# A decoder layer on one core: sends paced in fours, a quarter of the dense expert moved to the front, and a closing sum made by VectorE alone

## The chip, the core and the metric

The kernel runs on 1 core of a Trainium2 chip. The metric is the device time of one execution in microseconds (us); the time of a kernel is the median of its runs.

A core has five engines with a queue of instructions each: TensorE (PE in the profile, with its weight loads as PEld), VectorE (DVE), ScalarE (ACT), GpSimd (POOL) and SyncE (SP), which here only issues transfers. Matrix products land in PSUM; everything else lies in SBUF or in device memory (DRAM). Each queue is worked off in order, and an instruction whose input is not there holds up all that stand behind it.

## The reference, cut to what matters

One decoder layer over 16 x 64 = 1024 tokens of width 256, in float32: self-attention, cross-attention over a second sequence, and a mixture of experts, each behind a layernorm and added to x. Only the last part is touched:

```
xt = layernorm(x)                              # 1024 tokens x 256
scores = softmax(xt @ Wg.T)                    # 16 experts in 4 groups
best 2 groups by their maximum, in them the best 4 experts: topi, weights
h = silu(xt @ W1[e].T) * (xt @ W3[e].T)        # 176 wide, for each expert e
expert_out[e] = h @ W2[e].T
y = sum over e of expert_out[e] * combine[:, e]    # 0 where e was not chosen
z = (silu(xt @ Ws1.T) * (xt @ Ws3.T)) @ Ws2.T      # the shared expert, 352 wide
x = x + y + z
```

## The kernel before

**Tokens and tiles.** x stays in SBUF as eight tiles of 128 tokens (`x[0]` to `x[7]`, pairs in one buffer), or two halves of 512 tokens. A float32 product is made of three: each operand is split in a high part (a cast, by ScalarE) and a low part (the difference, by VectorE or GpSimd); `parts_of` makes both, at lines 112 and 113. Every matrix product of this part goes through the helper at line 104.

**Routing through DRAM.** Experts 0 to 14 take only tokens that chose them; 15, the last, is computed densely for all tokens. For each token tile and each of four choices, `send` (line 842) issues one indirect transfer on GpSimd that scatters 128 rows to slots of the DRAM table `xd`, 384 slots for an expert. That is 4 choices x 4 tiles x 2 halves = 32 sends. The framework would order writes to one table one behind the other; `side_by_side` declares each send independent of the ones before it. Expert e's load of its rows waits only for the sends of choices 0 to e (of all four from e = 3 on), since `expert_inputs` asks for `sent_for[k]` of those choices.

**One expert** (loop over e at the end of `decoder_layer`):
- `expert_weights`: SyncE loads 640 KB; ScalarE casts the high part (line 278), VectorE makes the low part (line 283), helped by GpSimd from e = 3 on. At most two raw weight tiles are alive.
- `expert_inputs`: SyncE loads 384 rows (tile `xr`, line 1255), PE transposes them (1265), `parts_of` makes `xs`.
- `expert_hidden`: 18 products of 384 columns ("up products"), silu (ScalarE, 1283 and 1286), product (VectorE, 1284 and 1287), parts `hp`.
- `send_outputs`: 15 products of 256 columns, copies to `y` (1299), three indirect transfers on GpSimd that scatter rows to the DRAM table `yd` (1304), by token and choice.

For e = 1 and 2 the hidden layer of expert e - 1 is put ahead of the inputs of expert e; later the inputs come first, so that PE always has an expert's rows ready. Weights of expert e are issued behind the last silu issued so far (`tc.issue_after(silus[-1])`); such calls only bind the order in which instructions are placed, and a scheduler with a model of its own places the rest. The order in each queue is then fixed.

**The dense expert.** Its weights are `w_last`. Half 0 is computed with the shared expert before the loop. Half 1 comes in two quarters of 256 tokens: `dense_hidden` (18 products of 256 columns and the steps of a hidden layer) and `dense_output` (10 products and two adds to x at line 952, `add_last`). Both quarters stand at the end: hidden of the first before expert 14's outputs, the rest after them.

**The end.** `load_outputs(k)` loads the rows of choice k from `yd`, four loads of 256 KB on SyncE (line 1320, tile `got`, nine buffers), once the sends that can hold rows of it have landed: choice 0 after expert 11, choice 3 after expert 14. `add_outputs` multiplies each of the eight tiles with its weight and adds it to x: two of three tiles by one VectorE instruction (line 1334), every third by ScalarE (1331, the multiplication) and GpSimd (1332, the addition). Then x goes out, eight stores, in turn from SyncE and ScalarE (1392).

Of the kernel before, what the change touches and what calls it, by code (L numbers as in the profile page):

```python
# [29 lines left out]
AF = mybir.ActivationFunctionType  # L30
ALU = mybir.AluOpType
# [11 lines left out]
E, INTER, NGRP, TOPK, TOPKG = 16, 176, 4, 4, 2  # L43
# [28 lines left out]
def decoder_layer(ctx: ExitStack, tc: tile.TileContext, a: dict, out: bass.AP):  # L72
    nc = tc.nc
# [17 lines left out]
    def av_tile():  # L91
        return ps_av.tile([128, 512], F32, tag="av", name="av")
# [18 lines left out]
    def parts_of(src, hi, lo, eng=None):  # L111
        nc.scalar.copy(hi, src)  # L112
        return (eng or nc.vector).tensor_tensor(lo, src, hi, ALU.subtract).ins
# [3 lines left out]
    x = [t[:, i, :] for t in x_pairs for i in range(2)]  # L117
# [122 lines left out]

    yd = dram.tile([(E - 1) * SLOTS + TOPK * NT, D], F32, tag="yd", name="yd")

    def side_by_side(sent, others):

        for other in others:
            tc.declare_no_dep(sent, other, reason="each writes rows of its own")
        others.append(sent)

    def behind(read, writes):
        for w in writes:  # L250
            tc.add_manual_dep(
                read,
                w.name,
                mybir.DependencyInfo(mybir.DependencyClass.Sync, mybir.DependencyReason.DATA),
                reason="it reads rows of each",
            )
# [29 lines left out]
    def expert_up(w, xs, n):  # L286


        ps = [mm_tile(cols=n) for _ in range(3)]
        return ps, [expert_up_part(k, w, xs, t) for k, t in enumerate(ps)][-1]  # L290
# [24 lines left out]
    with ExitStack() as attn:  # L315
# [410 lines left out]
        rows = [None, None]  # L726
        sent_rows, sent_for = [], [[] for _ in range(TOPK)]
# [108 lines left out]

        def send(half, choices=range(TOPK), waits=()):

            to = targets[half]
            for k in choices:  # L840
                for i in range(4):
                    sent = nc.gpsimd.indirect_dma_start(
                        out=xd[: TOPK * NT + (E - 1 - k) * SLOTS],
                        out_offset=bass.IndirectOffsetOnAxis(ap=to[:, k, i : i + 1], axis=0),
                        in_=rows[half][i // 2][:, i % 2, :],
                        in_offset=None,
                    ).ins
                    side_by_side(sent, sent_rows)
                    sent_for[k].append(sent)
                    behind(sent, waits)  # L850

# [107 lines left out]
        with (  # L959
# [109 lines left out]
            def dense_weights():  # L1069

                parts = [
                    xw.tile([128, 2, 2, 4 * HQ], F32R, tag=f"w_q{n}", name=f"w_last{n}")
                    .rearrange("p a b c -> p (a b c)")[:, :W_COLS]
                    for n in range(2)
                ]
                up = xb.tile([128, 3, 2, 2, DC], F32, tag="w_s", name="w_last_up")
                down = xb.tile([128, 2, D], F32, tag="w_o0", name="w_last_down")
                for t, cols in (
                    (up.rearrange("p a b c d -> p (a b c d)"), slice(0, W_UP)),
                    (down.rearrange("p a b -> p (a b)"), slice(W_UP, W_COLS)),  # L1080
                ):
                    nc.sync.dma_start(out=t, in_=a["W123"][E - 1][:, cols])
                    parts_of(t, parts[0][:, cols], parts[1][:, cols])
                return parts
# [18 lines left out]
            def dense_gated(g, up, g2, up2):  # L1103
                h_p = [
                    xa.tile([128, 512], F32R, tag=f"roped1{n}", name=f"dense1{n}", bufs=1)
                    for n in range(2)
                ]
                h_p.append(xa.tile([128, 512], F32R, tag="q_r", name="dense2"))
                nc.vector.tensor_tensor(g, up, g, ALU.mult)
                parts_of(g, h_p[0], h_p[1])  # L1110
                nc.vector.tensor_tensor(g2[:64], up2[64:], g2[64:], ALU.mult)
                parts_of(g2[:64], h_p[2][:64], h_p[2][64:])
                return h_p
# [15 lines left out]
            for n in range(len(units) + 2):  # L1129
# [5 lines left out]
                qd, half = units[min(n, len(units) - 1)]  # L1135
# [52 lines left out]
                if n == 8:  # L1188
                    w_last = dense_weights()
                    with after(exps[-1]):  # L1190
                        routed.append(weights_of_choices(0))
                if n == 9:
# [30 lines left out]
                    with after(aimed, placed):  # L1223
# [4 lines left out]
                        h_p = dense_gated(*dense_ups)  # L1228
# [9 lines left out]
    gated, up_done = [None], [None]  # L1238
# [34 lines left out]
    def expert_hidden(w, xs, n):  # L1273


        ps, up_done[0] = expert_up(w, xs, n)
        g, h, g2, h2 = (
            fh.tile([128, SLOTS], F32, tag=tag, name=tag)[:, :n] for tag in ("g", "h", "g2", "h2")
        )
        h_p = [  # L1280
            fh.tile([128, SLOTS], F32R, tag=tag, name=tag)[:, :n] for tag in ("hp0", "hp1", "hp2")
        ]
        nc.scalar.activation(g, ps[0], AF.Silu)
        nc.vector.tensor_tensor(h, ps[1], g, ALU.mult)
        parts_of(h, h_p[0], h_p[1])
        silus.append(nc.scalar.activation(g2[64:], ps[2][:64], AF.Silu).ins)
        nc.vector.tensor_tensor(h2[:64], ps[2][64:], g2[64:], ALU.mult)
        gated[0] = parts_of(h2[:64], h_p[2][:64], h_p[2][64:])
        return h_p
# [24 lines left out]
    def load_outputs(k):  # L1314

        tiles = []
        for n in range(NI // 2):
            t = fy.tile([128, 2, D], F32, tag="got", name="got", bufs=9)
            first = (E - 1) * SLOTS + (TOPK - 1 - k) * NT + n * 256
            got = nc.sync.dma_start(  # L1320
                out=t, in_=yd[first : first + 256].rearrange("(i p) d -> p i d", p=128)
            ).ins
            behind(got, returned)
            tiles.append(t)
        return tiles

    def add_outputs(k, got, cw):
        for i in range(NI):
            y, w = got[i // 2][:, i % 2], cw[i // 4][:, k, i % 4 : i % 4 + 1]
            if i % 3 == 2:  # L1330
                nc.scalar.activation(y, y, AF.Copy, scale=w)
                nc.gpsimd.tensor_tensor(x[i], x[i], y, ALU.add)
            else:
                nc.vector.scalar_tensor_tensor(x[i], y, w, x[i], ALU.mult, ALU.add)  # L1334

    def dense_hidden(w, half, n):
        return expert_hidden(w, [p[:, :, n * 256 : n * 256 + 256] for p in normed[half]], 256)

    def dense_output(w, h_p, half, n, add):
        for b in range(2):  # L1340
            ps = av_tile()[:, :D]
            expert_output(ps, w, h_p, slice(b * 128, b * 128 + 128))
            add(half, 2 * n + b, ps)
# [6 lines left out]
    ws, xs, hs, got = {}, {}, {}, {}  # L1350
    with tc.issue_after(lows[-1]), tc.issue_after(silus[-1]):
        ws[0] = expert_weights(a["W123"][0], nc.vector)
    for e in range(E + 1):
        if e in (1, 2):

            low = lows[-1]
            hs[e - 1] = expert_hidden(ws[e - 1], xs[e - 1][0], SLOTS)
        if e < E - 1:
            low = lows[-1]
            with tc.issue_after(up_done[0] if e in (1, 2) else low):  # L1360
                xs[e] = expert_inputs(e)
            if e >= 1:
                with tc.issue_after(low), tc.issue_after(silus[-1]):
                    ws[e] = expert_weights(a["W123"][e], nc.vector if e < 3 else nc.gpsimd)
        if e == 1:
            with tc.issue_after(gated[0]), tc.issue_after(silus[-1]):
                routed.append(weights_of_choices(1))
        if 0 <= e - 1 < E - 1 and e > 2:
            hs[e - 1] = expert_hidden(ws[e - 1], xs[e - 1][0], SLOTS)
        if e - 2 >= 0:  # L1370
            if e == E:

                with tc.issue_after(gated[0]):
                    h_p = dense_hidden(w_last, 1, 0)
            last = send_outputs(e - 2, ws.pop(e - 2), hs.pop(e - 2), xs.pop(e - 2)[1])
            if e - 2 == E - TOPK - 2:
                short = slots_are_short()
            k = e - 2 - (E - 1 - TOPK)
            if k >= 0:
                got[k] = load_outputs(k)  # L1380
    with ExitStack() as behind_last:
        for ins in (*last, gated[0]):
            behind_last.enter_context(tc.issue_after(ins))
        cw = [r[0] for r in routed]
        add_outputs(0, got[0], cw)
        dense_output(w_last, h_p, 1, 0, add_last)
        add_outputs(1, got[1], cw)
        dense_output(w_last, dense_hidden(w_last, 1, 1), 1, 1, add_last)
        for k in range(2, TOPK):
            add_outputs(k, got[k], cw)  # L1390
    for i in range(NI):
        (nc.sync if i % 2 == 0 else nc.scalar).dma_start(
# [10 lines left out]
    with tc.If(short > 0):  # L1403
        w_over = [weights_without_slot(half, routed[half][2]) for half in range(2)]
        with tc.For_i(0, E - 1, 1) as e:
            w = expert_weights(a["W123"][bass.ds(e, 1)].rearrange("o p c -> p (o c)"))
# [109 lines left out]
```

## Time and profile before

| what | us |
|---|---|
| median of 3 runs (572.08 to 573.05) | 572.2 |
| the profiled execution, its own time | 577.4 |
| its span | 575.5 |
| PE busy | 540.3 (94%) |
| DVE busy | 400.2 (70%) |
| ACT busy | 279.3 (49%) |
| POOL busy | 230.6 (40%) |
| mean granted clock of PE | 0.978 of full |

A line of the order of time gives the start, the time, the engine, the line of the kernel, the operation, what is written and read, how many follow each other, and in brackets how long the engine had been idle and what ended that. The durations in the trace come from one execution, which took 5.2 us more than the median. Transfers that an engine only issues don't count as its busy time.

### The profile page before, as it was taken

The page shows a single profiled execution, that of the slowest core. Times are in us where ns is not written, and L with a number is a line of the kernel's source. Part 1 is how long each engine was busy: PE and PEld are TensorE (multiplying, and loading weights), DVE is VectorE, ACT ScalarE, POOL GpSimd, SP SyncE. Part 2 cuts the span into 40 slices and gives each one's busy share as a digit, 9 for nine tenths or more (in the row PEclk, how much of TensorE's full clock was granted, in tenths as well). Part 3 has the DMA queues.
Part 4 walks back from the last instruction along what each step waited for, and adds up shares of the span by engine and source line. Part 5 has one row for each costly group of instructions (what it writes and reads, how often), then busy time and mean ns, then how long its engine had stood idle before and what let it go on. Part 6 is the DMA issues. An engine that isn't in the chain of part 4 may idle for free.

```text
span 575.5 us, 10603 instructions
## 1 busy us (share of the span) xinstructions
PE 540.3 (94%) x4013; PEld 446.7 (78%) x4013; DVE 400.2 (70%) x879; ACT 279.3 (49%) x524; POOL 230.6 (40%) x213
## 2 busy tenths in 40 slices
PE   7999999999999989999999999999999779999962
PEld 5889898888989876757778577685787669999951
DVE  6355566644655788848577586889777479999866
ACT  4677557575574431230432323152525187777551
POOL 4260500101001005426243444632544717888862
PEclk9999999999999999999999999999999789999995
DMA  8564431823200599482020000000511658777384
GB/s 227 145 166 146 111 109 39 227 86 112 75 1 1 167 250 308 111 239 52 2 70 1 8 1 1 0 31 0 188 50 68 202 169 285 240 245 238 122 279 152
DMA packets 56294, 70.83 MB, mean 123 GB/s; under 512 B 13872, under 2 KB 42768, under 8 KB 56240
## 3 DMA queue, kind: packets, MB, share of 16 engines
q1 hardware_dynamic: 51408, 58.71, 34.5%
q0 software_dynamic: 3696, 10.36, 4.7%
q10 hardware_dynamic: 1136, 1.05, 0.6%
q8 instruction: 33, 0.54, 0.4%
q14 instruction: 21, 0.17, 0.1%
HBM read 48.61 MB, written 21.86 MB: 122 GB/s over the span
## 4 chain that ended last, share of the span: by engine, by line
PE 81%; DVE 7%; issue 4%; DMA 3%; ACT 3%; POOL 1%; SPq 1%; DVEq 0%; ACTq 0%; POOLq 0%
PE mm L104 47%; PE mm L1005 7%; PE av L590 5%; PE av L104 5%; PE at L573 4%; PE at L343 3%; PE at L1028 2%; PE av L1041 2%; PE at L1265 2%; PE mm L439 2%; DMA bqkv<-in_bqkv 1%; PE mm L461 1%; DMA got<-yd 1%; DVE x L1334 1%; POOL roped L990 1%
## 5 line engine op out<-in xcount | busy, mean ns | idle before, releaser
L990 POOL TENSOR_TENSOR roped<-rt,rt 128x512 f32<-128x512 f32 x48 | 62.6, 1325 | 83.4 <-DVE rt L984 80.5
L984 DVE TENSOR_TENSOR rt<-mm,rope_q 128x512 f32<-128x512 f32 x96 | 61.4, 685 | 24.3 <-PE mm L104 23.6
L104 PE MATMUL mm<-xn,w_q 128*128 128x512 f32 x288 | 73.9, 403 | 0.5 <-ACT xn L222 0.5
L104 PEld LDWEIGHTS mm<-xn,w_q 128*128 128x128 f32 x288 | 52.2, 188 | 14.0 <-issue 1.8
L104 PE MATMUL mm<-xs,w 128*128 128x384 f32 x270 | 55.3, 354 | 7.0 <-ACT xs L112 5.8
L1304 POOL DMA_INDIRECT yd<-y,to x45 | 47.9, 1064 | 27.6 <-ACT y L1299 13.1
L104 PEld LDWEIGHTS mm<-xs,w 128*128 128x128 f32 x270 | 48.4, 198 | 9.0 <-ACT xs L112 6.6
L327 ACT ACTIVATE p<-p 128x512 f32<-128x512 f32 x32 | 20.1, 629 | 62.3 <-DVE p L326 62.3
L324 DVE TENSOR_REDUCE sm_m<-at 128x8 f32<-128x512 f32 x32 | 21.8, 680 | 37.1 <-PE at L573 36.2
L1005 PE MATMUL mm<-roped,w_s 128*64 128x512 f32 x192 | 46.4, 602 | 0.7 <-POOL roped L990 0.7
L522 POOL TENSOR_TENSOR wv<-code,scale 128x512 fp32r<-128x512 f32 x7 | 9.5, 1360 | 88.2 <-DMA scale<-in_scales 58.7
L613 DVE TENSOR_TENSOR x<-mm,x 128x256 f32<-128x256 f32 x64 | 26.0, 419 | 23.9 <-PE mm L104 21.9
L104 PE MATMUL mm<-wo,o 128*128 128x256 f32 x256 | 39.6, 295 | 0.0
L104 PE MATMUL av<-w,hp 128*128 128x256 f32 x225 | 35.2, 290 | 0.7 <-ACT y L1299 0.7
L104 PE MATMUL mm<-xn,wq 128*128 128x512 f32 x128 | 34.6, 405 | 0.7 <-ACT xn L222 0.5
L104 PE MATMUL mm<-wv,xn 128*128 128x256 f32 x256 | 35.2, 289 | 0.0
L104 PE MATMUL mm<-xn,wk 128*128 128x512 f32 x128 | 34.9, 404 | 0.0
L590 PE MATMUL av<-pt,v 128*128 128x128 f32 x256 | 34.5, 277 | 0.0
L104 PEld LDWEIGHTS mm<-wo,o 128*128 128x128 f32 x256 | 32.9, 190 | 1.5 <-issue 0.4
L590 PEld LDWEIGHTS av<-pt,v 128*128 128x128 f32 x256 | 32.0, 191 | 1.2
L104 PEld LDWEIGHTS mm<-wv,xn 128*128 128x128 f32 x256 | 31.8, 189 | 0.9
L104 PEld LDWEIGHTS av<-w,hp 128*128 128x128 f32 x225 | 30.6, 190 | 1.9 <-ACT y L1299 1.2
(216 smaller groups left out, 1145.8 us busy)
## 6 DMA issues: line engine op xcount, KB each, us to landing
w<-in_W SPq DMA_DIRECT2D x15, 640.0 KB
code<-in_codes SPq DMA_DIRECT2D x32, 256.0 KB
scale<-in_scales SPq DMA_DIRECT2D x32, 256.0 KB
xr<-xd SPq DMA_DIRECT2D x15, 408.0 KB
xd<-zeros SPq DMA_DIRECT2D x8, 720.0 KB
yd<-zeros SPq DMA_DIRECT2D x8, 512.0 KB
got<-yd SPq DMA_DIRECT2D x16, 256.0 KB
wq<-in_Wq SPq DMA_DIRECT2D x4, 512.0 KB
```

The lines of the kernel that those rows point to most:

```text
L104: m = nc.tensor.matmul(ps, lhsT=l, rhs=r, start=(n == 0), stop=(n == len(pairs) - 1))
L324: nc.vector.tensor_reduce(m, sc, AX.X, ALU.max)
L327: exps.append(nc.scalar.activation(p, p, AF.Exp, scale=scale).ins)
L343: last = nc.tensor.transpose(ps[:, 2 * n : 2 * n + 2, :].rearrange("p a q -> p (a q)"), pn[:, 2 * n : 2 * n + 2, :].rearrange("p a k -> p ...
L439: nc.tensor.matmul(ps[:, c * DCQ : (c + 1) * DCQ], lhsT=wq[:, h, c * 128 : (c + 1) * 128], rhs=wkq[:, h, :], start=True, stop=True,)
L573: nc.tensor.matmul(sc[par * 64 : par * 64 + 64, 2 * g + pp, :], lhsT=qk[0][:, b * S : (b + 1) * S], rhs=qk[1][:, b * S : (b + 1) * S], sta ...
L590: nc.tensor.matmul(av[:, k * 128 : (k + 1) * 128], lhsT=v[:, i, k0 : k0 + HD], rhs=pt[:, i].rearrange("p a q -> p (a q)"), start=True, sto ...
L613: nc.vector.tensor_tensor(x[i], ps, x[i], ALU.add)
L984: nc.vector.tensor_tensor(mt, ps3, rope_table(t, 2 * ab + k), ALU.mult)
L990: nc.gpsimd.tensor_tensor(r.rearrange("p (b s) -> p b s", s=S), one, two, op)
L1005: nc.tensor.matmul(ps[h // 2][(h % 2) * 64 : (h % 2) * 64 + 64], lhsT=w_s[:, t, blk, ab, :], rhs=roped[2 * t + ab], start=first[h], stop=l ...
L1304: sent = nc.gpsimd.indirect_dma_start(out=yd[: (E - 1) * SLOTS + min(TOPK, E - 1 - e) * NT], out_offset=bass.IndirectOffsetOnAxis(ap=to[:, ...
```

## The change

- `send`: for half 1 and choices 1 to 3, each of the four sends keeps its dependence on the last send before the four. It waits until that one has landed. (The sends of half 0, and choice 0 of half 1, are as before.)
- The loop: expert 2's hidden layer also comes ahead of expert 3's inputs, so expert 3's rows are used later.
- The first quarter of half 1 of the dense expert: its hidden layer is placed behind expert 0's up products, its output products and adds ahead of expert 0's outputs. Only the second quarter is left at the end, its hidden layer before expert 14's outputs, its output after them.
- `add_outputs`: all eight tiles by VectorE's one instruction; no ScalarE multiplication, no GpSimd addition.
- `load_outputs`: of the last choice, two of the four loads are issued by ScalarE instead of SyncE.

```
-    def side_by_side(sent, others):
+    def side_by_side(sent, others, landed=()):
         for other in others:
-            tc.declare_no_dep(sent, other, reason="each writes rows of its own")
+            if other not in landed:
+                tc.declare_no_dep(sent, other, reason="each writes rows of its own")
         others.append(sent)
...
             for k in choices:
+                landed = sent_rows[-1:] if half and k else ()
                 for i in range(4):
...
-                    side_by_side(sent, sent_rows)
+                    side_by_side(sent, sent_rows, landed)
...
-            got = nc.sync.dma_start(
+            got = (nc.scalar if k == TOPK - 1 and n % 2 else nc.sync).dma_start(
...
     def add_outputs(k, got, cw):
         for i in range(NI):
             y, w = got[i // 2][:, i % 2], cw[i // 4][:, k, i % 4 : i % 4 + 1]
-            if i % 3 == 2:
-                nc.scalar.activation(y, y, AF.Copy, scale=w)
-                nc.gpsimd.tensor_tensor(x[i], x[i], y, ALU.add)
-            else:
-                nc.vector.scalar_tensor_tensor(x[i], y, w, x[i], ALU.mult, ALU.add)
+            nc.vector.scalar_tensor_tensor(x[i], y, w, x[i], ALU.mult, ALU.add)
...
     for e in range(E + 1):
-        if e in (1, 2):
+        if e in (1, 2, 3):
             low = lows[-1]
             hs[e - 1] = expert_hidden(ws[e - 1], xs[e - 1][0], SLOTS)
+            if e == 1:
+                with tc.issue_after(up_done[0]):
+                    h_p = dense_hidden(w_last, 1, 0)
         if e < E - 1:
             low = lows[-1]
-            with tc.issue_after(up_done[0] if e in (1, 2) else low):
+            with tc.issue_after(up_done[0] if e in (1, 2, 3) else low):
                 xs[e] = expert_inputs(e)
...
-        if 0 <= e - 1 < E - 1 and e > 2:
+        if 0 <= e - 1 < E - 1 and e > 3:
             hs[e - 1] = expert_hidden(ws[e - 1], xs[e - 1][0], SLOTS)
         if e - 2 >= 0:
             if e == E:
                 with tc.issue_after(gated[0]):
-                    h_p = dense_hidden(w_last, 1, 0)
+                    h_p = dense_hidden(w_last, 1, 1)
+            if e == 2:
+                dense_output(w_last, h_p, 1, 0, add_last)
             last = send_outputs(e - 2, ws.pop(e - 2), hs.pop(e - 2), xs.pop(e - 2)[1])
...
-        add_outputs(0, got[0], cw)
-        dense_output(w_last, h_p, 1, 0, add_last)
-        add_outputs(1, got[1], cw)
-        dense_output(w_last, dense_hidden(w_last, 1, 1), 1, 1, add_last)
-        for k in range(2, TOPK):
+        dense_output(w_last, h_p, 1, 1, add_last)
+        for k in range(TOPK):
             add_outputs(k, got[k], cw)
```

## The prediction

> **What bounds the kernel now.** I read the page first, for the share of each engine in the chain that ended last; then busy time by stretches of ten microseconds from 430 us on, because every edit lies in the mixture-of-experts part; then the order of time around the start of the experts and around the end; last the two programs' orders of instructions, engine by engine.
>
> ```profile
> span 575.5 us, 10603 instructions
> ...
> PE 540.3 (94%) x4013; PEld 446.7 (78%) x4013; DVE 400.2 (70%) x879; ACT 279.3 (49%) x524; POOL 230.6 (40%) x213
> ...
> PE 81%; DVE 7%; issue 4%; DMA 3%; ACT 3%; POOL 1%; SPq 1%; DVEq 0%; ACTq 0%; POOLq 0%
> ```
>
> TensorE is the bound as a whole. By stretches:
>
> ```profile
> 480.00:490.00 10.00, 10.00 (x74) 10.00 (x73) 9.18 (x17) 8.40 (x18) 6.63 (x7) 1.00 0.83 277
> ...
> 530.00:540.00 10.00, 10.00 (x67) 9.66 (x66) 9.36 (x17) 6.38 (x16) 8.68 (x7) 1.00 0.39 141
> ...
> 560.00:570.00 10.00, 3.21 (x10) 2.36 (x10) 9.84 (x19) 2.59 (x6) 4.05 (x5) 0.50 0.62 195
> ```
>
> The columns are length, then PE, weight loads, DVE, ACT, POOL, the granted clock, DMA share and GB/s. From 475 to 550 PE has no room: whatever makes the experts start later comes through one to one. After 560 DVE is the full engine. So there are two places to cost: the start of the experts, and the end. The start, in order of time:
>
> ```profile
> 454.54 4.82 PE L104 MATMUL mm<-xs,w 128*128 128x384 f32 x18 [1.45 <-ACT xs L112]
> ...
> 459.19 0.82 PE L1265 MATMUL at<-ident,xr 128*128 128x128 f32 x6
> ...
> 460.57 0.48 ACT L1286 ACTIVATE g<-mm 64x384 f32<-64x384 f32 x1 [1.33 <-PE at L1265]
> 461.08 1.26 ACT L278 CAST w<-w 128x1280 fp32r<-128x1280 f32 x1
> ...
> 462.37 1.56 DVE L283 TENSOR_TENSOR w<-w,w 128x768 fp32r<-128x768 f32 x2 [0.72 <-ACT w L278]
> 462.70 0.48 ACT L112 CAST xs<-at 128x384 fp32r<-128x384 f32 x1 [0.37 <-remote]
> ...
> 463.24 0.79 PE L104 MATMUL mm<-xs,w 128*128 128x384 f32 x3 [3.23 <-ACT xs L112]
> ...
> 463.96 0.56 DVE L113 TENSOR_TENSOR xs<-at,xs 128x384 fp32r<-128x384 f32 x1
> ...
> 464.57 3.25 PE L104 MATMUL mm<-xs,w 128*128 128x384 f32 x9
> ...
> 471.41 0.80 PE L104 MATMUL mm<-xs,w 128*128 128x384 f32 x3 [1.10 <-ACT xs L112]
> ...
> 472.70 0.95 POOL L1304 DMA_INDIRECT yd<-y,to  x1 [11.50 <-ACT y L1299]
> ```
>
> Expert 0's 18 up products end at 459.4. Expert 1's begin at 463.2 and in bulk at 464.6: PE stands for 3.23 us while ACT makes g2 of expert 0, casts w1 (1.26 us), then xs, and DVE makes w1's low part (1.56 us), then xs's. Expert 2 has such a hole of 1.10 us. The clock, us by us:
>
> ```profile
> 450.00:451.00 1.00, 0.32 (x2) 0.32 (x3) 1.00 (x3) 0.00 (x0) 0.85 (x1) 0.91 0.41 148
> ...
> 464.00:465.00 1.00, 0.91 (x6) 0.71 (x5) 1.00 (x3) 0.98 (x2) 0.00 (x0) 0.73 0.36 78
> 465.00:466.00 1.00, 1.00 (x4) 1.00 (x4) 0.97 (x3) 0.68 (x1) 0.00 (x0) 0.50 0.93 307
> ```
>
> It halves twice, 450.8 to 457.6 and 464.5 to 467.9, each time after a thin stretch. The end:
>
> ```profile
> 552.59 3.65 DVE L1334 SCALAR_TENSOR_TENSOR x<-got,cw,x 128x256 f32<-128x256 f32 x9
> ...
> 558.62 0.85 DVE L1334 SCALAR_TENSOR_TENSOR x<-got,cw,x 128x256 f32<-128x256 f32 x1 [2.38 <-DMA got<-yd]
> ...
> 561.20 1.42 DVE L1334 SCALAR_TENSOR_TENSOR x<-got,cw,x 128x256 f32<-128x256 f32 x2
> ...
> 563.39 1.83 DVE L1334 SCALAR_TENSOR_TENSOR x<-got,cw,x 128x256 f32<-128x256 f32 x2
> ...
> 566.12 0.51 ACT L1331 ACTIVATE got<-got,cw 128x256 f32<-128x256 f32 x1 [1.00 <-DMA got<-yd]
> ```
>
> Nine adds follow each other in 3.65 us, so one per 0.40. Later the same form takes 0.7 to 1.0 where POOL adds beside it. DVE ends at 571.2; stores and closing take 4.3 more.
>
> **The end, step by step.** DVE's 18.6 us from 552.6 to 571.2 are: 24 choice adds and 4 dense adds at 0.40 (11.2); four steps of the second quarter's hidden layer at 0.42 (1.7); 2.4 waiting for a load; and some 3.2 of instructions stretched beside POOL (0.85 for 0.40; 1.42 and 1.83 for 0.80; a hidden step of 0.97 for 0.42; about 0.5 in the last rows). Sum 18.5. The change adds 8 choice adds, removes 2 dense adds and the four hidden steps, and takes POOL away: 34 at 0.40 is 13.6, so DVE could end at 566.2. It is then not DVE but the last choice's loads that end last. They wait for expert 14's sends (SyncE issues from 561.0 to 562.9); the third has landed at 566.1, the fourth, issued 0.46 later, by about 566.7 (estimate). Two adds more: 567.6 against 571.2, a gain of 3.6. I take 3.5. The range is 2.0 (the loads come 1.5 later) to 5.0 (the sends leave earlier, as 18 products no longer follow expert 14's outputs on PE). The nine load buffers cost nothing: the last load needs the 24th DVE instruction, 552.6 + 9.5 = 562.1, no later than its issue now. ACT's eight multiplies (0.51 each) and POOL's eight adds (0.78) go from engines with room.
>
> [...] The four issues stand 0.46 apart, while the transfers run until 566.7. [...] By the issue rows alone the fourth load could gain 0.9[...]. I take 0.
>
> **The quarter of the dense expert.** Its 18 up products (2.3 us in the trace, before 554.9) now stand between expert 0's and expert 1's transposes. That looks like PE's hole, but on ACT the cast of w1 waits for the last silu issued, which is now the quarter's own g2: ACT's order is g, g2, hp, g (dense), hp, g2 (dense), then the cast, one dense cast (0.41), xs. So the cast follows the 18 products instead of running beside them. The bulk of expert 1's products moves from 464.6 by 2.3 + 0.4 to 467.3: most of the hole moves instead of being filled. What lies behind on DVE is w1's low part and one dense step, and PE waits for both.
>
> How late they end depends on the clock. Before: 9 products at half clock (3.25 us), then 6 in 1.2, end 469.2. After: 15 products from 467.3. [...] 15 at 0.175 is 2.6, end 469.9, or +0.7. The row disagrees: at 450.8 the clock halved after one 1.6 us gap, and it stayed halved past 454 although about 60% of those 3.4 us were busy. The stretch 464.5 to 467.9 will hold some 2.2 busy us of 3.4, so I take half clock for one more stretch, to 471.3: 11 products at 0.36, 4 at 0.18, end 472.1, or +2.9. If the clock returns at 467.9 it is +1.1. Range 0.7 to 2.9; I take the row.
>
> The quarter's ten output products (five took 0.75) run beside the waits for xs. Its two adds (0.48 each) stand on DVE ahead of w2's low parts; PE has 12 output products meanwhile: +0.4 (0 to 1).
>
> **Fourth rows later.** Expert 2's up products now come before expert 3's transposes, so expert 3 gets a hole as experts 1 and 2 have: ACT g, g2, cast of w3, xs in a row. Nothing in the trace shows it at expert 3; nearest are 1.10 at expert 2 and 3.23 at expert 1, with 8 output products to fill. I take 1.5, near the first of the two (0 to 3.2).
>
> **Sends in fours.** Twelve sends of half 1 wait on POOL for the landing of the last send of the choice before. Before, 16 leave 1.27 us apart until 461.2. A landing takes 2.0 us (the first choice: POOL done 444.5, read at 446.5) to 3.7 (the third: 456.1, 459.8), so three waits put the end near 469 to 470. Behind them POOL has nothing until 472.7, idle for 11.5: that cover hides it. On SyncE w2's load moves ahead of expert 1's rows, which leave near 454.7 instead of 452.4 and land before 460, for a use after 461.6. Expert 2's rows leave near 463 (459.8), used at 472. Expert 3's leave near 471 (463.5), used after 478, and behind them w3, at 471.5 (464.4), cast near 479. I cost all at 0 (below nothing by up to 1, if thinner DMA traffic helps; above by up to 3, if w3 or rows come late, each us one to one).
>
> **Sum.** Start +2.9 + 0.4 + 1.5 = +4.8; end -3.5; together +1.3. Against the profiled execution, 575.5 span and 577.4 in all, that is 576.8 and 578.7. The profiled run is 5.2 above the median of 572.2; I carry the difference over: 573.5.
>
> **The rivals.** (1) The clock decides the other way: it returns at 467.9, or never drops. The start costs 1.1 + 0.4 + 1.5 = 3.0 or, with no drop, 2.6; the end gives 3.5 to 5: 0.5 to 2.4 faster, 569.8 to 571.7, middle 570.8. For it: the dense products do thicken the stretch before; against it: the two drops in the rows. It decides if expert 1's products end before about 470.8 (469.2 and the 1.6 that the other terms leave of the 3.5). (2) The last loads bind harder: on the busy DMA (0.9 and more from 553 to 560) DVE waits longer for them and the end gives only 2: +2.8, 575.0. For it: DVE already waits 2.38 there. (3) The fours bring w3 or the rows late: +3 on top, 576.5. Against it: covers of 7 us. (4) The two queues and the fours do nothing that can be seen; this is in the sum already.
>
> **How the numbers follow.** Forecast 0.44, rival 1 0.34, rival 2 0.13, rival 3 0.09. The forecast's own range is 572 to 575; about a third of it and a little of rival 1 lie within 0.2% (1.1 us, about what a measurement of this kernel tells from no change). So faster 0.33, same 0.18, slower 0.49. Cases of both signs are in: 569.5 to 576.8 leaves out the far ends of rivals 1 and 3.
>
> **What would show it.** Right: the cast of w1 stands behind the dense g2 on ACT, PE's hole before expert 1 is still about 3 us in all, the clock is at 0.50 beyond 468, expert 14's sends end 4 to 6 us after 557.1, DVE runs at 0.40 per add with no stretched rows, and its last add comes about 10.5 us after expert 14's last send, not 14. Wrong: expert 14's sends end within 2 us of 557.1 (the start is too dear in my sum), or the last adds wait for loads by more than 3 us (the end is too cheap).

## The result, and the profile after

| what | before | after |
|---|---|---|
| median, us (7 runs each, one chip) | 572.29 | 575.66 |
| ratio, 95% interval | | 1.0056 (1.0037 to 1.0075) |
| the profiled execution, own time, us | 577.4 | 574.3 |
| its span, us | 575.5 | 572.5 |

The change costs 3.2 us (0.0056 of 572.3). The forecast was slower, 573.5 with a range of 569.5 to 576.8, so sign and range hold; the size does not (1.3 us forecast). But the two traces say the opposite of the medians: the one of after is 3.0 us shorter. Before's trace lies 5.1 us above its median, after's 1.3 below. This is the first thing to clear up. From the page of after:

```profile
span 572.5 us, 10584 instructions
...
PE 535.1 (93%) x4013; PEld 441.3 (77%) x4013; DVE 401.6 (70%) x887; ACT 275.7 (48%) x516; POOL 226.2 (40%) x205
...
PE 75%; DMA 7%; POOL 6%; issue 5%; DVE 4%; ACT 2%; SPq 0%; DVEq 0%; POOLq 0%; ACTq 0%
```

DMA and POOL have 13% of the chain that ended last, where before they had 4%: landings of transfers and the sends now stand on the path. By stretches of 10 us, PE is as full as before in the middle. After 560 it does nothing, and DVE is no longer full (6.63 of 10 us, 9.84 before):

```profile
480.00:490.00 10.00, 10.00 (x73) 9.93 (x72) 8.74 (x17) 8.83 (x20) 7.09 (x7) 1.00 0.90 305
530.00:540.00 10.00, 10.00 (x69) 9.97 (x69) 9.75 (x18) 7.05 (x17) 8.74 (x7) 1.00 0.39 136
560.00:570.00 10.00, 0.00 (x0) 0.00 (x0) 6.63 (x17) 0.00 (x0) 0.00 (x0) 0.50 0.75 246
```

The start of the experts after the change, in order of time:

```profile
455.28 2.31 PE L104 MATMUL mm<-xn,w_last 128*128 128x256 f32 x18
...
457.63 0.38 ACT L1290 ACTIVATE g<-mm 64x256 f32<-64x256 f32 x1 [0.44 <-issue]
...
457.91 0.85 PE L1269 MATMUL at<-ident,xr 128*128 128x128 f32 x6 [0.32 <-DMA xr<-xd]
458.03 1.26 ACT L280 CAST w<-w 128x1280 fp32r<-128x1280 f32 x1
...
461.86 2.87 PE L104 MATMUL mm<-xs,w 128*128 128x384 f32 x15
...
466.26 0.84 PE L1269 MATMUL at<-ident,xr 128*128 128x128 f32 x6 [1.53 <-DMA xr<-xd]
...
469.81 1.14 POOL L1308 DMA_INDIRECT yd<-y,to  x1 [2.15 <-ACT y L1303]
```

The quarter's 18 products follow expert 0's at once. The cast of w1 stands on ScalarE behind the quarter's g2 (457.63), as predicted, and the bulk of expert 1's products starts at 461.86. New is the 1.53 us that PE stands for expert 2's rows at 466.26. The clock by the same microseconds that were shown of before:

```profile
450.00:451.00 1.00, 0.83 (x6) 0.64 (x6) 1.00 (x4) 0.25 (x1) 0.70 (x2) 1.00 0.14 48
464.00:465.00 1.00, 0.73 (x5) 0.41 (x3) 0.71 (x4) 0.89 (x1) 0.89 (x1) 1.00 0.88 272
465.00:466.00 1.00, 0.00 (x0) 0.00 (x0) 0.07 (x1) 0.96 (x3) 0.69 (x2) 1.00 0.95 362
```

It is full throughout the start, even in a microsecond in which PE does nothing. The end:

```profile
551.52 2.86 DVE L1334 SCALAR_TENSOR_TENSOR x<-got,cw,x 128x256 f32<-128x256 f32 x7
...
555.13 0.96 POOL L1308 DMA_INDIRECT yd<-y,to  x1 [0.30 <-issue]
...
561.12 0.88 DVE L1334 SCALAR_TENSOR_TENSOR x<-got,cw,x 128x256 f32<-128x256 f32 x2 [1.10 <-DMA got<-yd]
562.20 5.77 DVE L1334 SCALAR_TENSOR_TENSOR x<-got,cw,x 128x256 f32<-128x256 f32 x14 [0.20 <-DMA got<-yd]
```

Seven adds take 2.86 us and fourteen 5.77: 0.41 each, nothing is stretched any more. DVE's last add ends at 567.97, 11.9 us after expert 14's last send (556.09). DVE stands for loads at 561 and still has 14 adds to do from 562.2 on.

### The profile page after: what moved, and what is told of

Read it like the earlier page. It is cut to its first block, busy times and chain, and to the rows that moved or that the text cites. A ratio compares the mean times of both kernels' runs of the same rounds, so it can differ in the third digit from the quotient of the medians.

```text
span 572.5 us, 10584 instructions
## 1 busy us (share of the span) xinstructions
PE 535.1 (93%) x4013; PEld 441.3 (77%) x4013; DVE 401.6 (70%) x887; ACT 275.7 (48%) x516; POOL 226.2 (40%) x205
## 4 chain that ended last, share of the span: by engine, by line
PE 75%; DMA 7%; POOL 6%; issue 5%; DVE 4%; ACT 2%; SPq 0%; DVEq 0%; POOLq 0%; ACTq 0%
PE mm L104 43%; PE mm L1009 7%; PE av L592 5%; POOL xd L846 4%; PE av L104 4%; PE at L575 4%; PE at L345 2%; PE at L1032 2%; PE mm L441 2%; PE av L1045 2%; DMA got<-yd 2%; DMA xd<-rows,to 2%; PE at L1269 1%; DMA x<-in_x 1%; PE mm L463 1%
## 5 line engine op out<-in xcount | busy, mean ns | idle before, releaser
L104 PEld LDWEIGHTS mm<-xn,w_q 128*128 128x128 f32 x288 | 52.2, 188 | 14.1 <-issue 1.8
L104 PE MATMUL mm<-xs,w 128*128 128x384 f32 x270 | 53.1, 341 | 3.7 <-issue 2.2
L104 PEld LDWEIGHTS mm<-xs,w 128*128 128x128 f32 x270 | 45.7, 188 | 5.7 <-issue 3.2
```

The lines of the kernel that those rows point to most:

```text
L104: m = nc.tensor.matmul(ps, lhsT=l, rhs=r, start=(n == 0), stop=(n == len(pairs) - 1))
```

## The experiments

**How the traces are compared.** Everything before the first send of half 1's rows (call it S) is the same in all kernels, but differs between the chips used by some 2 us (S at 436.7 to 439.6). So times are counted from S, in two pieces. The first runs from S to expert 14's first send to `yd`; it is called the start, since the middle runs alike (54.8 to 56.0 us from expert 4's first send to expert 14's in all traces). The second, the end, runs from there to the end of the span. The last column is PE's time at half clock between S and 482. Times are in us.

| kernel | ratio to before | 95% interval | S to expert 14 | end | half clock |
|---|---|---|---|---|---|
| before, first trace | | | 113.18 | 22.97 | 10.2 |
| before again | 0.9997 | 0.9989 to 1.0006 | 108.77 | 22.32 | 0 |
| after, first trace | 1.0056 | 1.0037 to 1.0075 | 112.54 | 20.36 | 0 |
| after again | 1.0054 | 1.0033 to 1.0074 | 113.55 | 21.15 | 3.4 |
| before + VectorE's adds | 1.0009 | 0.9992 to 1.0026 | 111.29 | 22.06 | 6.8 |
| before + later fourth rows | 1.0032 | 1.0019 to 1.0045 | 111.32 | 22.01 | 3.4 |
| before + early quarter | 1.0046 | 1.0029 to 1.0063 | 111.58 | 22.97 | 3.4 |
| before + fours | 1.0107 | 1.0086 to 1.0128 | 115.17 | 22.23 | 10.2 |
| after - fours | 1.0044 | 1.0029 to 1.0060 | 112.05 | 21.23 | 0 |
| after - early quarter | 1.0039 | 1.0027 to 1.0051 | 110.52 | 23.30 | 3.4 |
| after - later rows | 1.0059 | 1.0040 to 1.0079 | 115.81 | 20.82 | 3.4 |
| after - fours - quarter | 1.0051 | 1.0033 to 1.0069 | 109.82 | 23.01 | 0 |
| after - second queue | 1.0058 | 1.0039 to 1.0077 | 113.49 | 19.18 | 3.4 |
| after - fours, cast of w1 first | 1.0047 | 1.0026 to 1.0068 | 112.86 | 21.33 | 3.4 |

A trace is one execution, and most executions of a kernel lie within 1 to 2 us of their median, a few further off. The ratios carry the verdicts; the traces show the places.

**Before again.** No edit.

> The kernel before, unchanged, for a second trace of it. The profiled execution of before (577.4 us) lies 5.1 above its own median, that of after (574.3) 1.4 below its. Theory A: the two half-clock stretches at 450.8-457.6 and 464.5-467.9 belong to that one execution; a new one has full clock until the end, a span near 570 to 571, sends of expert 14 that end near 552 to 553 and a last add near 566. Rival: the stretches are in every execution of before and the new trace repeats them (span 575, sends end at 557). The ratio is 1.000 within 0.2%.

Theory A held, on a chip on which everything lies 2.4 us earlier. The trace of before, a second time, at the start and one of the microseconds shown earlier:

```profile
453.40 1.26 ACT L278 CAST w<-w 128x1280 fp32r<-128x1280 f32 x1
453.87 0.85 PE L1265 MATMUL at<-ident,xr 128*128 128x128 f32 x6 [1.01 <-DMA xr<-xd]
...
456.89 1.84 PE L104 MATMUL mm<-xs,w 128*128 128x384 f32 x9 [0.55 <-DVE xs L113]
...
458.81 1.21 PE L104 MATMUL mm<-xs,w 128*128 128x384 f32 x6
...
464.56 0.96 POOL L1304 DMA_INDIRECT yd<-y,to  x1 [6.20 <-ACT y L1299]
```

```profile
465.00:466.00 1.00, 0.83 (x8) 0.63 (x7) 1.00 (x3) 0.00 (x0) 0.69 (x2) 1.00 0.95 311
```

Nine products of expert 1 take 1.84 us, not 3.25, and expert 14 is reached 108.77 us after S instead of 113.18. The 4.4 us that the first trace lost are not a property of the kernel. The medians of before on the chips used are 569.8 to 572.7. Less 1.8 outside the span, less S and an end of 22.3, the usual execution of before needs 108.7 to 109.4. The mean granted clock says the same: it was 0.978 in the first trace, and of the 92 other executions of before and of before again two have 0.978 or less; their median is 0.984.

Not all of the 4.4 us is the clock's. Before it halved at 450.8, the first trace was already late:

```profile
449.55 0.48 DVE L952 SCALAR_TENSOR_TENSOR x<-av,cl,x 128x256 f32<-128x256 f32 x1 [3.07 <-PE mm L104]
...
450.68 1.13 PE L104 MATMUL mm<-ws,sh 96*128 96x256 f32 x4 [1.65 <-issue]
```

This add of VectorE reads dense products that began at 446.77, 2.78 us before it. In before again the same add comes 0.79 us after their begin (445.20 and 444.41). Behind it VectorE makes the low part of `sh` until 450.63, and PE stands 1.65 us before the products that read it. Expert 0's products begin 15.1 us after S, against 11.7 in before again. How much of the loss is this late add and how much the half clock that followed is not shown.

Against before again the two traces of after lose 3.8 and 4.8 us at the start and gain 2.0 and 1.2 at the end.

**After again.** No edit.

> After, unchanged, for a trace beside the other parts on one chip. From the parts so far (without the fours 1.0044, without the early quarter 1.0039) I expect 1.0056, that is 573.0 where before is 569.8, the first send of expert 0's outputs some 2.6 later after the first send of half 1's rows than in before, and the last add 11.9 after expert 14's last send. Rival: on this chip the change costs nothing at the start and the ratio is 1.000.

1.0054, as expected. The two traces of after differ in two places: this one has a half-clock stretch late in the start, from 477 (the start is 1.0 us longer), and it takes 12.6 us from the last send to the last add, where the first took 11.9.

**The early quarter**, out of after, and alone on before (with the old adds, all in one run at the end):

```
-            if e == 1:
-                with tc.issue_after(up_done[0]):
-                    h_p = dense_hidden(w_last, 1, 0)
...
-            if e == 2:
-                dense_output(w_last, h_p, 1, 0, add_last)
```

> After, with both quarters of the dense expert at the end as before, all adds on VectorE still. Theory A: 18 products at 0.13 and 10 at 0.15 (3.8 us) leave the start, where they run beside waits only in part, and w1's cast no longer stands behind the dense g2: the experts begin 2 to 3 us sooner; VectorE then has 40 steps in the end in place of 34 (+2.4), but the loads of the last choice come sooner too; net 0 to 1 us faster than after, ratio 1.004 to 1.0056. Rival (the quarter is what pays, it fills a hole): 2 us slower than after, ratio 1.009.

> Before, with the early quarter of the dense expert alone (the old adds of three engines, one queue, no fours, rows as before). Theory A (3.7 us of TensorE's work go to where TensorE is the bound and about 1.3 of them fill a stand; the end gives 1.2 to 2 back): expert 4's outputs leave 56.1 us after the first send, no half clock at the start; ratio 1.000 to 1.002. Rival (the quarter is most of the 3.3 us lost): 1.004 to 1.005.

Out of after: 1.0039, about 1 us less than 1.0055 and just under what theory A allowed; the intervals overlap, so this difference is not clear of noise. Alone: 1.0046, 2.6 us slower, and the rival's number, not the one I had put first. At the start PE was at half clock once, from 465, where I had expected none. What I had wrong is the end, which gives nothing at all (22.97) when ScalarE and GpSimd still add. The order of time at the end of before with the early quarter alone:

```profile
562.39 0.51 ACT L1335 ACTIVATE got<-got,cw 128x256 f32<-128x256 f32 x1 [1.17 <-DMA got<-yd]
...
563.03 0.73 POOL L1336 TENSOR_TENSOR x<-x,got 128x256 f32<-128x256 f32 x1 [0.82 <-ACT got L1335]
563.09 1.34 DVE L1338 SCALAR_TENSOR_TENSOR x<-got,cw,x 128x256 f32<-128x256 f32 x2 [0.21 <-DMA got<-yd]
```

All three engines stand for the same loads, GpSimd by way of ScalarE: with DVE lightened, the loads bind the last adds. Yet these end 12.6 us after expert 14's last send, about as in after (11.9 and 12.6) and earlier than in before (14.1 and 13.7). The time is lost behind them. Each engine's queue closes with an instruction that the trace records as DRAIN and that the views leave out. GpSimd's ends 6.4 us or more after its last work in all fourteen traces. Here it runs from 564.12 to 570.48, while SyncE's, behind its waits for the stores, is over at 567.68; the span ends at 571.3. In the two traces of before GpSimd's DRAIN ends 0.5 and 0.9 us ahead of SyncE's, and in after, where GpSimd does not add, 9.3 us ahead. So with GpSimd still adding, the early quarter moves the adds forward but not the end.

**The adds on VectorE alone**, on before:

```
-            if i % 3 == 2:
-                nc.scalar.activation(y, y, AF.Copy, scale=w)
-                nc.gpsimd.tensor_tensor(x[i], x[i], y, ALU.add)
-            else:
-                nc.vector.scalar_tensor_tensor(x[i], y, w, x[i], ALU.mult, ALU.add)
+            nc.vector.scalar_tensor_tensor(x[i], y, w, x[i], ALU.mult, ALU.add)
```

> Before, with all adds on VectorE and nothing else. The prediction put the end at 3.5 less, of which the quarter (six VectorE steps, 2.5 us) leaves only with the early quarter. Theory A (the last choice's loads and VectorE's 40 steps bind equally; POOL's contention gone is worth what eight more adds cost, 3.2): same as before, ratio 0.999 to 1.001. Rival (contention with POOL is dear, as the prediction's sum has it): 1 to 2 us faster, ratio 0.997.

1.0009: nothing that can be told from no change. This fits theory A (eight more adds on DVE, 3.2 us, cost what is gained where DVE's instructions are no longer stretched beside GpSimd's, some 3.2 us in the first trace of before), but it does not separate the two. So each half of the end's change is worth nothing alone. With the adds on VectorE but both quarters at the end, the last add still comes 12.9 to 14.4 us after the last send (three traces); with the quarter early but GpSimd adding, GpSimd's DRAIN holds the end. Only with both does the end become shorter: 19.2 to 21.3 us in six traces, against 22.0 to 23.0 in the four with the end of before, 1.7 us between the means.

**The later fourth rows**, alone on before, and out of after:

```
-        if e in (1, 2):
+        if e in (1, 2, 3):
...
-        if 0 <= e - 1 < E - 1 and e > 2:
+        if 0 <= e - 1 < E - 1 and e > 3:
```

(and the same in the condition for `up_done`).

> Before, with the later place of the fourth rows alone. Theory A (hidden: in the part that has it without fours and quarter, expert 4's outputs leave 53.9 us after the first send of half 1, as in the undisturbed trace of before, 53.75): 1.000. Rival (the prediction's 1.5 us for a hole before expert 3): 1.0026; with the 2.4 us that lie between the part with later rows and two queues (1.0051) and before with VectorE's adds (1.0009), 1.004.

> After, with expert 3's transposes ahead of expert 2's products again, as before. Theory A (the hole before expert 3's products costs about what the prediction put, 1.5): ratio 1.003. Rival (with sends in fours expert 3's rows are late, so the later place hides their wait and the edit pays for itself): TensorE stands for expert 3's rows with expert 2's products behind them, 1 to 3 us slower than after, ratio 1.008 to 1.011.

Alone: 1.0032, 1.8 us; the prediction's 1.5 stands, and "hidden", which I had read off one trace, falls. The hole itself, before expert 3's products, is 0.8 us in this trace and in the one without fours and early quarter; where the rest of the 1.8 lies is not shown. Out of after: 1.0059, no gain. There the edit pays back what it costs, because the fours bring rows and w3 late. From the order of time of after without the later rows:

```profile
470.37 0.52 PE L1269 MATMUL at<-ident,xr 128*128 128x128 f32 x3 [1.91 <-DMA xr<-xd]
...
474.08 1.26 ACT L280 CAST w<-w 128x1280 fp32r<-128x1280 f32 x1 [6.17 <-DMA w<-in_W]
...
475.76 0.45 PE L104 MATMUL mm<-xs,w 128*128 128x384 f32 x1 [1.83 <-ACT xs L112]
```

Expert 3's transposes stand in front of expert 2's products and hold up both, and w3, whose load waits on SyncE behind those rows, makes ScalarE stand 6.17 us.

**The sends in fours**, out of after, and alone on before:

```
-                landed = sent_rows[-1:] if half and k else ()
+                landed = ()
```

> After, with the sends of half 1 not waiting for the choice before. In after, expert 2's rows leave behind the late sends and TensorE stands 1.53 us for them before expert 2's transposes; w3 comes 0.51 and w4 1.58 us late for their casts. Theory A (the fours cost, since the cover was used up): 1.5 to 2.5 us faster than after, ratio to before 1.002, and the stand at 466 is gone. Rival (fours cost nothing; the early quarter and the later rows cost all): the same as after, ratio 1.0056.

> Before, with the sends in fours alone. Theory A (SyncE's loads of rows 1 to 3 each stand for the landing, and nothing covers it: expert 1's rows 1.8 later than before, expert 3's late by 3, as in after with the earlier rows, where expert 1's outputs came 3 to 4 us later): 1.004 to 1.008, with a half clock in the stand. Rival (the prediction's cover of 11.5 us on GpSimd hides it): 1.000.

Out of after: 1.0044, 0.6 us less, between what the two theories gave and inside both intervals of after, so at most a weak sign. The stand of 1.53 us for expert 2's rows is gone in the trace, but another is in its place:

```profile
465.75 0.86 PE L104 MATMUL av<-w,hp 128*128 128x256 f32 x5 [2.11 <-DVE x L956]
```

These are expert 0's output products, and they stand for VectorE's add of the early quarter. They begin 28.36 us after S; in after, behind the stand for the rows, 28.35. So at this place the fours are hidden behind the early quarter.

Alone on before: 1.0107, 6.1 us slower, more than even theory A gave. The order of time of before with the fours alone:

```profile
452.53 0.96 POOL L844 DMA_INDIRECT xd<-rows,to  x1 [3.45 <-DMA xd<-rows,to]
...
470.81 0.87 PE L1267 MATMUL at<-ident,xr 128*128 128x128 f32 x3 [4.79 <-DMA xr<-xd]
471.33 3.23 PE L104 MATMUL mm<-xs,w 128*128 128x384 f32 x9
```

GpSimd stands 1.73, 3.45 and 1.72 us for the three landings. SyncE's loads of the rows leave later for it, and PE stands 2.52, 1.15 and 4.79 us for the rows of experts 1, 2 and 3, where before again has 1.01, 0.60 and none. After the last of these PE works at half clock (nine products in 3.23 us). This half clock does not come and go: all six executions of this kernel have a mean granted clock of 0.973 to 0.980, and the 17 of before beside them 0.982 to 0.988.

What makes the fours nearly free in after is that the early quarter and the later rows move the use of the rows back. Either of the two is cover enough for most of it: after without the early quarter is at 1.0039, after without the later rows at 1.0059. Those two edits cost time, and the fours ride on their cost.

**Neither fours nor early quarter.** What is left of after are the later rows, VectorE's adds and the second queue.

> After without fours and without the early quarter: what is left is the later place of the fourth rows, the adds on VectorE, and two queues for the last loads. With the fours but without the quarter it was 1.0039, where expert 1's rows came 2.79 us late (1.01 in before). Theory A (fours cost 1.4 to 1.8 where no quarter covers them): 1.001. Rival (the fours are hidden and the later rows cost the 2 us): 1.0035 to 1.004.

1.0051, on the rival's side and above it. The start of its trace is only 1.05 us over that of before again, the end 0.7 over. With 1.0032 for the later rows and 1.0009 for the adds the interval (1.0033 to 1.0069) can be met; I don't read more out of it.

**One queue for the last loads**, in after:

```
-            got = (nc.scalar if k == TOPK - 1 and n % 2 else nc.sync).dma_start(
+            got = nc.sync.dma_start(
```

> After, with all of the last choice's loads on SyncE again. From expert 14's first send to the end of the span it was 22.05 us in before with VectorE's adds (one queue), and 23.0 to 23.3 in the two parts that have both dense quarters at the end and two queues. Theory A (ScalarE's queue for two of the loads costs about 1 us): ratio 1.0035 to 1.004. Rival (the prediction's 0; that difference is scatter of the landing): 1.0055, the same as after.

1.0058 against 1.0054 and 1.0056: the rival holds, the second queue does nothing. Its trace even has the shortest end:

```profile
558.59 6.64 DVE L1334 SCALAR_TENSOR_TENSOR x<-got,cw,x 128x256 f32<-128x256 f32 x16 [0.51 <-DMA got<-yd]
```

The 1 us that had made me suspect the queue is no more than these traces scatter.

**The cast of w1 first.** After without the fours, with the dense hidden layer moved behind the lines that make expert 1's inputs and weights:

```
-            if e == 1:
-                with tc.issue_after(up_done[0]):
-                    h_p = dense_hidden(w_last, 1, 0)
...
             if e >= 1:
                 with tc.issue_after(low), tc.issue_after(silus[-1]):
                     ws[e] = expert_weights(a["W123"][e], nc.vector if e < 3 else nc.gpsimd)
+            if e == 1:
+                with tc.issue_after(up_done[0]):
+                    h_p = dense_hidden(w_last, 1, 0)
```

> After without the fours, and the dense quarter's up products issued after expert 1's transposes and w1's cast, so that they fill TensorE's stand before expert 1 while ScalarE casts. Against after without the fours (1.0044). Theory A (the cast of w1 behind the dense silus is what the start costs): expert 1's products in bulk come 2 us sooner, ratio 1.0005 to 1.0015. Rival (the late place of w1's cast does not matter, the holes before experts 2 and 3 take what is left): within 0.5 us of 1.0044.

1.0047: no gain on 1.0044, theory A falls. From its order of time:

```profile
455.97 1.26 ACT L280 CAST w<-w 128x1280 fp32r<-128x1280 f32 x1
...
456.80 2.40 PE L104 MATMUL mm<-xn,w_last 128*128 128x256 f32 x18
...
461.24 4.78 PE L104 MATMUL mm<-xs,w 128*128 128x384 f32 x17 [1.87 <-ACT g L1287]
```

The cast is now over at 457.23, 0.43 us after the dense products begin. But expert 1's bulk stands for ScalarE's silu of the quarter (`g`) and starts 22.16 us after S; with the cast behind (after without the fours) it was 22.23. The stand only changes its releaser. In this trace the silu itself came late: at 460.80, after 1.99 us without work, though the dense products had ended at 459.20. This placement also pushed expert 0's output products behind expert 2's up products, and the clock halved for 3.4 us. So what the cast alone would bring in an unchanged order is not shown.

No part and no combination was faster than before.

## Why the prediction was right or wrong, point by point

| step | predicted, us | measured, us |
|---|---|---|
| early quarter at the start (2.9 + 0.4) | +3.3 | +2.2 (after - fours against after - fours - quarter, both at full clock) |
| later fourth rows | +1.5 | +1.8 (ratio, alone), +1.05 (trace of after - fours - quarter) |
| fours | 0 | +0.6 by ratio, 0.5 by traces at full clock; +6.1 without the other two |
| start, all together | +4.8 | +3.8 and +4.8 (two traces of after against before again) |
| end | -3.5 | -2.0 and -1.2 (the same traces), -1.7 (means of six and four traces) |
| sum | +1.3 | +3.2 (ratio) |

- **The base.** The step that failed first is the last one, "I carry the difference over". The traced execution of before had lost 4.4 us at the start, to a late result and to the half clock. I took this for the kernel's own time and set the change's steps against it. The prediction's own test shows the error: expert 14's sends should end 4 to 6 us after 557.1 and ended at 556.1, "the start is too dear". Against before again they do come later, by 3.8 and 4.8 us after S. So the start's +4.8 was about right as a difference to a usual execution, and that is in part luck: of its steps the quarter was put too high and the fours too low, and the half clock was assumed on both sides of the sum. What made the forecast too low is the end.
- **The clock.** I had two ends for expert 1's products, full clock throughout (the +0.7 of the range) and half clock until 471.3 (+2.9), and took the second as an estimate from the first drop in the trace of before (450.8 to 457.6, two stretches of 3.4 us). No trace of after has it there (after again once, later, from 477). Of the seven traces without the early quarter four have a half-clock stretch that begins between 450 and 461; of the six in which the quarter directly follows expert 0's products none has. Rival 1 had the clock right, and still its 569.8 to 571.7 did not come, since before usually has the full clock there too: expert 1's 15 products start 2.4 us later after S than in before again (22.2 against 19.85) and are done 2.1 us later (25.1 against 23.0).
- **The quarter fills little of the hole.** Right in the main. 18 and 10 products are 3.8 us of work; 2.2 of them appear as delay. The cast of w1 follows the dense g2, as said, but the experiment with the cast first shows that this is not the only thing behind the stand. The hole was also smaller than read: from expert 0's up products (in after, the quarter's) to expert 1's bulk PE is idle 3.3 us in the first trace of before, 1.9 in before again and 1.7 in after, where the prediction named "still about 3 us" as a sign of being right.
- **Fourth rows later.** Right in size (1.8); of the hole that was to make it, 0.8 us is seen.
- **Fours.** Nearly hidden, as said (the last send ends at 467.7, not at 469 to 470), but the named cover was the wrong one. GpSimd's 11.5 us without work hide nothing, as GpSimd is not the one that waits: SyncE's loads and PE behind them do. In before again these 11.5 us are 6.2, and the fours alone cost 6.1. Expert 2's rows were "used at 472" in my sum; in after PE is ready for them at 464.7, and they come 1.5 us late. That they cost little there is the doing of the other two edits.
- **The end.** The term that was mis-sized. The adds run at 0.41, as said, where before had 0.7 to 1.0 beside GpSimd's. But I counted DVE's 34 adds without any wait and let only two of them follow the last landing. DVE stands for loads at 558.75, 561.12 and 562.2, 1.7 us in all, and 0.6 for PE (dense products). From 562.2 on it works without a stop, so there its 14 adds bind and not the last load. In after again ten adds follow the last wait for a load, at 565.18. From the last send to the last add it takes 10.9 to 12.7 us in the six traces with this end, not 10.5. Rival 2 had the end's size (it gives only 2), and with the base corrected its sum, +2.8, is nearest to the 3.2 measured. Its mechanism shows only in part: DVE waits 1.7 and 1.9 us for loads in the two traces of after, not longer than the 2.4 before. The sum also called the adds of ScalarE and GpSimd work of engines with room; by the closing DRAIN, GpSimd had 0.5 to 0.9 us of room at the very end.
- **Two queues.** Nothing (1.0058 with one queue, 1.0056 and 1.0054 with two), as the prediction took it, by estimate.

What stays open: the two traces of after give 1.8 and 3.6 us over before again, and one trace each does not narrow it further. The parts don't add up either (1.8 + 2.6 + 6.1 + 0.5 alone, 3.2 together); the traces show for the fours that one part covers another. By ratio the early quarter costs 2.6 alone and nothing that can be told in after without the fours (1.0044 with it, 1.0051 without), where its end gives back what its start costs.

## What to carry to other kernels

Before working out a change on a trace, ask whether its execution is a usual one. When it lies several us off the median, find what it lost, and set the sum against the rest. Work moved from a place with a slack engine to one where that engine is the bound costs its full length minus the hole it really fills (here 3.8 us of products cost 2.2), and the hole must be free on every engine that the work passes, not on one. A wait that is hidden has to be covered where its consumer stands; test it alone, and it shows what covered it. When an end gets shorter on one engine, look at what each of the others still has to close (here GpSimd, 2.8 us after SyncE with the early quarter alone).

## What the runs showed of the hardware that was not expected

**Half clock comes in stretches of 3.4 us, and not in every execution.** In ten of the fourteen traces PE was halved at the start, for 3.4, 6.8 or 10.2 us in all; the same kernel had 10.2 in one execution and none in another. Only the fours alone had a low clock in every execution (0.973 to 0.980 in six). One row of before with VectorE's adds, from the windows of one microsecond:

```profile
453.00:454.00 1.00, 1.00 (x5) 1.00 (x5) 0.15 (x2) 0.00 (x0) 0.70 (x2) 0.50 0.76 122
```

PE had been busy 0.47, 0.58 and 0.65 of the three microseconds before; before again stood at 0.13 and 0.72 near the same place (from 453 to 455) and kept its clock at 1.00. What decides which execution is halved is not shown. So one trace doesn't tell what a thin stretch costs: before lost 4.4 us in one execution, together with a late result, and nothing in another.

**A PE result can be seen late.** In after again, at 554.64, ScalarE copies expert 14's last output tile after 2.49 us without work, though the products had ended at 552.2. After without fours and quarter shows 3.29 us before the silu at 554.02, whose products had ended at 551.2. The profile names no releaser but a remote one. VectorE's add at 449.55 in the first trace of before is of the kind, some 2 us later than in before again, and there a half clock followed. These places lie where sends and loads run; the cause was not tried.

**GpSimd closes slowly.** Its closing DRAIN ends 6.4 to 8.4 us after its last work in the fourteen traces, and where its last work is one of the closing sum's adds it takes 6.36 us each time (567.83 to 574.19 in the first trace of before). It ends 2.8 us after SyncE's with the early quarter alone, and 1.4 us after it in the trace of the fours alone; there it decides when the kernel ends.
